# First-pass maxima and early projections of two sixteen-head attention stages placed in the mixture stage ahead

## The chip, the core and the metric

The kernel runs on one core of a Trainium2 chip. The metric is the device time of one execution in microseconds (us), the median of several. TensorE is PE in the profile (PEld its weight loads), VectorE is DVE, ScalarE ACT, GpSimd POOL, SyncE SP; SP issues nearly all DMAs.

## The reference

Twelve residual stages work on one activation x of 2048 tokens by 128 channels, in four layers: half a feed-forward, an attention, half a feed-forward. Each stage normalises x first.

```python
x = x + 0.5 * ffn(layernorm(x)); x = x + attn(layernorm(x)); x = x + 0.5 * ffn(layernorm(x))
```

Layer 0 (ffn0, attn0): capacity routing over 8 experts, causal attention with 8 heads of 16. Layer 1 (ffn1, attn1): every token goes through a shared and eight gated experts, `silu(x @ wg) * (x @ wu) @ wd`, weighted by a top-2 softmax; full attention with 16 heads of 8. Layer 2 (ffn2, attn2): x is quantised in blocks of 32 to a 6-bit float grid and multiplied by a quantised weight; full attention with 16 heads of 8 and rotary angles. Layer 3 (ffn3, attn3): ternary weights; causal attention with 16 heads of 64. The sixteen-head stages of this change are attn1 and attn2:

```python
attn = softmax(einsum('bqhd,bkhd->bhqk', q, k) * dh**-0.5); out = einsum('bhqk,bkhd->bqhd', attn, v) @ Wo
```

## The kernel before, in words

x lies in SBUF in four chunks of 512 tokens. Each stage is a Python generator `main` with a small `pre` that fetches weights. A tile scheduler orders the instructions of each engine by a simulated readiness and by the order in which they were traced; `tc.high_priority()` lifts instructions, `in_order` and `keep_in_program_order` (in flash: `pe`) pin them behind others. Each engine then runs its list strictly in order.

Overlap of stages is written by hand in `Stage`. `io.upcoming()` prepares the next stage (its pool in SBUF, its weights, its generator), `io.mark(c)` says that chunk c of x is final, and `io.lead(us)` takes us off what the next stage still owes (`due`); when nothing is owed, the next stage does one step, until it yields True ("led"). Pools grow from the left end of SBUF for even stages and from the right for odd ones.

The mixture `ffn1` goes over 4 chunks x 9 experts. For each expert `up` makes two double-bank products in PSUM, `pg` and `pu` (12 matmuls of 512 columns in all, with a high and low split), ACT makes the Silu (L715), DVE multiplies (L717); `down` of the expert before makes 16 matmuls (L725) and DVE adds them with the gate to x (L735). At expert 4 the `front` of the next chunk is made. `io.lead(4.3)` stands once in each expert of chunks 2 and 3. `pg`, `pu` and the first-pass scores `s1` of flash share one PSUM tag of two double banks (`banks`).

The attention of `packed` treats 4 heads as a group: 4 groups x 4 query chunks are 16 iterations of `flash`. Stream A (L1049 on) makes the first-pass scores of an iteration: for 4 row blocks and 4 key chunks two pairs each, 32 pairs of matmuls of 32 rows by 512 (L1069), each pair followed by a maximum over 512 keys (L1087, one DVE reduction for two heads). `put_max` then turns the maxima into two more rows of the query. Stream B makes the second-pass scores (L1190), exponentials (L1199) and the product with the values (L1136). B starts an iteration when A has finished it, so the first iteration's 32 reductions stand ahead of every exponential.

Before flash, `packed` makes for chunks 0 to 2, one chunk after another as x becomes final: `front` (normalise, transpose, split), `queries_or_keys(1, c)` (keys; the queries of chunk 0 too), each a step of a lead. In attn1 these steps fall into the mixture ahead (ffn1). In attn2 the stage ahead is `ffn2`, whose last chunk makes eight leads (`io.here()`), so they fall beside its last quantisation. Once the stage itself runs, `kms` and `qts` are allocated in the pool `att`, filled by POOL, and filled by DMA with the stacked high and low parts (`stack_k`, `stack_q`, L1379), and at the first maxima `hook` makes the last chunk's keys (L1330, L1331).

`ffn2` runs per chunk: layer norm on ACT, `quantised` (L776 to L793, mostly DVE), transpose, product, addition into x (L834). Its chunks 0 to 2 are led by ffn1.

Of the kernel before, what the change touches and what calls it, by code (L numbers as in the profile page):

```python
# [64 lines left out]
def tile_macaron(ctx: ExitStack, tc: tile.TileContext, a: dict, out: bass.AP, stages=STAGES):  # L65
# [598 lines left out]
    def ffn1(io, k, w, early):  # L664
# [35 lines left out]
        with tc.tile_pool(name="f1", bufs=1) as pool, tc.tile_pool(name="f1w", bufs=1) as pool_w:  # L700
# [42 lines left out]
            for c in range(NC):  # L743
                xT, gate = cur
                for n, e in enumerate(order):
                    h = up(e, xT)
                    if n + 2 < len(order):
                        expert(order[n + 2])
                    if last is not None:
                        down(*last)  # L750
                    last = c, e, h, gate
                    if n == 4 and c + 1 < NC:
                        cur = front(c + 1, pool)
                    if n == 0 and c:
                        io.mark(c - 1)
                    if c > 1:
                        io.lead(4.3)
                if c == 0:
                    io.upcoming()
# [3 lines left out]
    def quantised(src, pool, tag, bufs=1):  # L763
# [5 lines left out]
        def new(name, m=n):  # L769
            return pool.tile([P, m], F32, name=name, tag=tag + name, bufs=bufs)  # L770
# [25 lines left out]
    def pre_ffn2(k, pool):  # L796
        if k == 0:
            w = fetch(pool, "l2w", 0, C)
            wqT.append(const.tile([P, P], F32, name="wqT"))
            q = quantised(w, pool, "w")  # L800
# [6 lines left out]
    def ffn2(io, k, w, early):  # L807
        bufs = 2 if k == 0 else 1
        half_bias = early.tile([P, C], F32, name="half_bias")
        nc.vector.tensor_scalar_mul(half_bias, row("bias2"), 0.5)  # L810
        for c in range(NC):
# [7 lines left out]
            q = quantised(xn.rearrange("p i c -> p (i c)"), early, "x", bufs)  # L819
# [5 lines left out]
            qT = early.tile([P, CH], F32, name="qT", tag="qT", bufs=bufs)  # L825
# [9 lines left out]
            io.mark(c)  # L835
            if c < NC - 1:
                yield 1.0
                stats_of[c] = statistics_of(xs[c])

# [130 lines left out]
    def flash(io, pool, early, its, nh, causal, scale, s1, s2, pv_mm, put_max, begin, finish, poll=None,  # L970
              on_exp=None, split_at=1, fill=None, leads=None, hook=None, flush=True, order=None):
# [30 lines left out]
        if halved:  # L1002

            halves = {}
            for name in ("ident", "maskq", "maskk"):
                raw = pool.tile([P, 2, P], F32, name="halfraw", tag="halfraw", bufs=2)
# [5 lines left out]
                halves[name] = pool.tile([P, 2, P], BF16, name="half" + name)  # L1012
# [11 lines left out]
        if tiled and causal:  # L1024
            junk = pool.tile([P, CH], F32, name="junk")
            strip = pool.tile([P, CH], F32, name="strip")
# [22 lines left out]
        def stream_a():  # L1049
            for n, (g, qc) in enumerate(its):  # L1050
                begin(n)
                nk = chunks(qc)
                npair = (nk + 1) // 2
                mp = pool.tile([P, TC, nh, NC], F32, name="mp", tag="mp", bufs=3)
                for pi in range(npair):
                    for r in range(TC):
                        before = hook(n, pi, r) if hook is not None else None
                        if pi == r == 0 and before is None:
                            before = last_top.get(n - 1)
                        for kc in range(2 * pi, min(2 * pi + 2, nk)):  # L1060
                            for j0 in range(0, nh, 2):
# [14 lines left out]
                                with tc.high_priority():  # L1076
# [17 lines left out]
                mx = pool.tile([P, TC, nh], F32, name="mx", tag="mxa", bufs=3)  # L1094
# [140 lines left out]

        while alive[0] and pos[0] < end[0]:
            step_a()
# [58 lines left out]
    def packed(io, early, hd, causal, scale, project, w, wv, wo, bias=None):  # L1296
# [45 lines left out]

        for c in range(1 if causal else NC - 1):
# [8 lines left out]
            if causal:  # L1352
                values(c)
        yield True

        with tc.tile_pool(name="att", bufs=1) as pool, tc.tile_pool(name="far", bufs=1) as far:
            tops = []
# [3 lines left out]
            vts = []  # L1361
# [3 lines left out]
            os = [  # L1365
                (far if causal else early).tile([P, TC, C], F32, name=f"o{c}", tag=f"o{c}")
                for c in range(NC)
            ]

            n_km, n_qt = 2 * NC, 5 if causal else 3  # L1370
            kms = [pool.tile([P, nq, CH], F32R, name=f"km{i}") for i in range(n_km)]
            qts = [pool.tile([P, nq, CH], F32R, name=f"qt{i}") for i in range(n_qt)]
            km, qt, q2, vt = {}, {}, {}, {}
            turn, held_by = [0], []

            def rows_of(dst, srcs, o):

                for t, s in enumerate(srcs):
                    nc.sync.dma_start(  # L1379
                        out=dst.rearrange("(d t) n -> d t n", t=4)[:, t].bitcast(F32),  # L1380
                        in_=s[o : o + per * hd, :].bitcast(F32),
                    )

            def stack_k(g, c):
                t = kms[(g * NC + c) % n_km if not causal else g * NC + c]
                h, l = parts[c][1]
                for i in range(nq):
                    rows_of(t[:, i, :], (h, l, h), (g * nq + i) * per * hd)
                km[g, c] = t

            def stack_q(g, c):
                h, l = parts[c][0]
                t = qts[turn[0] % n_qt]
                turn[0] += 1
                held_by.append((g, c))
                assert turn[0] <= n_qt or held_by[-1 - n_qt] in q2
                for i in range(nq):
                    rows_of(t[:, i, :], (h, h, l), (g * nq + i) * per * hd)
                qt[g, c] = t

            def stack_v(g, c):
                vt[g] = vts[g % 2]
                nc.vector.tensor_copy(
                    slots(vt[g])[:, c * TC : (c + 1) * TC, :, :hd],
                    vall[c][:, :, g * 4 * hd : (g + 1) * 4 * hd].rearrange(
                        "p i (j d) -> p i j d", j=4
                    ),
                )

            if causal:  # L1410
                its = [(g, c) for c in range(NC) for g in range(n_groups)]
            else:
                its = [(g, c) for g in range(n_groups) for c in range(NC)]
            size = [((4 * c + 2.5) if causal else 4 * NC) * CH * 4 for _, c in its]
            leads = even(size) if causal else None
            keyed = [0]

            def steps_of(i):

                if not x_parts[i]:  # L1420
                    xn = layer_norm(i, False)
                    yield
                    front(i, xn)
                    yield
                    queries_or_keys(1, i)
                    if causal:
                        queries_or_keys(0, i)
                        yield
                        values(i)
                        yield  # L1430
                for g in range(2 if causal else 1):
                    stack_k(g, i)
                    if causal:
                        stack_v(g, i)
                        queue(its.index((g, i)))
                        yield

            def onward(c):

                if keyed[0] > c:  # L1440
                    return False
                if not making:
                    making.append(steps_of(keyed[0]))
                if next(making[0], True):
                    making.pop()
                    keyed[0] += 1
                return True

            making = []

            def ensure(c):
                while onward(c):
                    pass

            def queue(n):

                if n < len(its) and its[n] not in qt:
                    c = its[n][1]
                    if not parts[c][0]:
                        queries_or_keys(0, c)  # L1460
# [833 lines left out]
```

## Time and profile before

| | us |
|---|---|
| median of 3 runs | 3757.37 |
| lowest and highest | 3753.88, 3758.66 |
| profiled execution | 3769.46 |
| its span, first to last instruction | 3767.7 |
| first mixture, first to last Silu start | 638.5 to 810.9 |
| first exponentials of attn1 | 881.8 |
| second mixture, first to last Silu start | 1524.0 to 1696.6 |
| first exponentials of attn2 | 1788.4 |

Over the whole span PE is busy 91%, DVE 76%, ACT 54%, POOL 22%. In an answer by order of time a line gives the start, the length, the engine, the line of the program, the operation, what is written from what with its shape, and how many equal instructions were merged; in brackets stands how long the engine was idle before, and who released it. A busy PE is not PE at its peak. "PEclk" is the granted share of TensorE's full clock.

### The profile page before, as it was taken

What the parts mean: (1) busy time and instruction counts of PE and PEld (TensorE: products, weight loads), DVE (VectorE), ACT (ScalarE), POOL (GpSimd) and SP (SyncE); (2) the same over time, 40 slices, a digit from 0 to 9 for tenths busy, and PEclk for the clock granted to TensorE, in tenths of its full rate; (3) what the DMA queues carried; (4) which work ended last, traced back from release to release, by engine and by line L of the source; (5) the groups of instructions that cost most, each with busy time, mean ns of one, the idle gap of its engine ahead of it and who ended that gap; (6) DMA issues with size and microseconds to landing.
All of it is one profiled execution on the core that took longest, in us unless ns stands there. A gap on an engine that the chain in (4) does not pass through costs nothing. (4 is left out here: it accounts for less than half of the span.)

```text
span 3767.7 us, 64628 instructions
## 1 busy us (share of the span) xinstructions
PE 3420.8 (91%) x25325; PEld 1846.5 (49%) x25325; DVE 2870.9 (76%) x4793; ACT 2036.2 (54%) x3838; POOL 828.8 (22%) x830
## 2 busy tenths in 40 slices
PE   7679987978999999996999999888999999999989
PEld 5543356863333333783333333366444444444458
DVE  6488555768999998668899999654777877788862
ACT  3246732325888888421788888732333444444442
POOL 1511124110000000112000000142555445533341
PEclk9779988987999999996999999998899999999999
DMA  3311023000000000102000000012443232221010
GB/s 104 83 49 29 9 81 95 4 26 5 12 12 14 8 3 1 35 1 70 10 14 6 16 5 4 15 46 75 140 147 112 97 106 97 89 63 52 24 34 12
DMA packets 124689, 170.18 MB, mean 45 GB/s; under 512 B 25120, under 2 KB 52514, under 8 KB 124384
## 3 DMA queue, kind: packets, MB, share of 16 engines
q1 hardware_dynamic: 121824, 160.80, 13.7%
q0 software_dynamic: 2560, 5.25, 0.9%
q8 instruction: 199, 3.26, 0.3%
q14 instruction: 106, 0.87, 0.1%
HBM read 101.25 MB, written 45.87 MB: 39 GB/s over the span
## 5 line engine op out<-in xcount | busy, mean ns | idle before, releaser
L1087 DVE TENSOR_REDUCE mp<-s 128x2 f32<-128x1024 f32 (+3 forms) x1440 | 1625.7, 1181 | 88.5 <-PE s L1069 68.1
L1199 ACT ACTIVATE pt<-s 128x512 f32<-128x512 f32 (+1 forms) x2368 | 1220.7, 601 | 216.4 <-PE s L1190 141.8
L1190 PE MATMUL s<-q,km 32*128 32x512 f32 (+2 forms) x2368 | 733.6, 491 | 28.6 <-ACT pt L1199 18.7
L1136 PE MATMUL pv<-pt,v 128*32 128x256 f32 (+1 forms) x8568 | 730.9, 413 | 22.9 <-ACT ov L1577 11.2
L1069 PE MATMUL s<-km,qt 32*128 32x512 f32 (+3 forms) x2368 | 620.0, 507 | 61.1 <-DVE mp L1087 37.1
L1190 PEld LDWEIGHTS s<-q,km 32*128 32x128 f32 (+1 forms) x2368 | 324.1, 184 | 531.6 <-issue 341.3
L1179 ACT ACTIVATE pt<-s 128x512 f32<-128x512 f32 (+3 forms) x640 | 306.2, 530 | 355.7 <-PE s L1171 212.8
L143 POOL TENSOR_TENSOR rs<-rs,minus_half 128x4 f32<-128x4 f32 x56 | 57.5, 1026 | 1543.7 <-DVE rs L142 1542.7
L1993 DVE TENSOR_TENSOR sum<-sum,pt 128x512 f32<-128x512 f32 (+3 forms) x328 | 259.4, 805 | 89.9 <-ACT pt L1179 88.3
L1136 PEld LDWEIGHTS pv<-pt,v 128*32 128x32 f32 x8568 | 169.1, 108 | 316.4 <-issue 146.3
L1171 PE MATMUL s<-q,k 64*128 64x512 f32 (+3 forms) x1920 | 300.0, 403 | 14.7 <-ACT pt L1179 10.4
L1136 PE MATMUL pv<-pt,latv 128*64 128x512 f32 (+3 forms) x1280 | 310.4, 564 | 1.3 <-ACT pt L1179 1.3
L1993 POOL TENSOR_TENSOR sum<-sum,pt 128x512 f32<-128x512 f32 (+1 forms) x200 | 265.6, 1328 | 181.5 <-ACT pt L1179 177.0
L1069 PEld LDWEIGHTS s<-km,qt 32*128 32x128 f32 (+1 forms) x2368 | 236.4, 191 | 124.1 <-DVE mp L1087 82.3
L1171 PEld LDWEIGHTS s<-q,k 64*128 64x128 f32 x1920 | 161.8, 188 | 224.8 <-issue 137.3
L715 ACT ACTIVATE sg<-pg 128x1024 f32<-128x1024 f32 x72 | 73.9, 1027 | 174.4 <-PE pg L229 158.8
L1069 PE MATMUL s<-k,q 64*128 64x512 f32 (+3 forms) x640 | 133.7, 433 | 19.0 <-DVE mp L1087 18.6
L1791 DVE TENSOR_TENSOR rot<-rot,tab 128x512 f32<-128x512 f32 x128 | 87.7, 685 | 74.2 <-PE rot L229 38.4
L725 PEld LDWEIGHTS pd<-l1d,h 128*128 128x128 f32 x1152 | 139.3, 192 | 5.6
L725 PE MATMUL pd<-l1d,h 128*128 128x128 f32 x1152 | 140.1, 275 | 0.0
L717 DVE TENSOR_TENSOR h<-pu,sg 128x1024 f32<-128x1024 f32 x72 | 87.9, 1220 | 60.6 <-PE pu L229 55.7
L1171 PE MATMUL s<-q,two 64*128 64x512 f32 (+3 forms) x640 | 128.0, 368 | 0.0
(575 smaller groups left out, 4696.7 us busy)
## 6 DMA issues: line engine op xcount, KB each, us to landing
tab<-in_l3rope SPq DMA_DIRECT2D x66, 256.0 KB
q<-q SPq DMA_DIRECT2D x32, 512.0 KB
k<-k SPq DMA_DIRECT2D x32, 512.0 KB
l0e<-in_l0e SPq DMA_DIRECT2D x32, 256.0 KB
q<-h SPq DMA_DIRECT2D x32, 256.0 KB
q<-rot SPq DMA_DIRECT2D x32, 256.0 KB
k<-h SPq DMA_DIRECT2D x32, 256.0 KB
k<-rot SPq DMA_DIRECT2D x32, 256.0 KB
```

Of the source, the lines that this page charges most:

```text
L715: nc.scalar.activation(sg, pg, AF.Silu)
L717: nc.vector.tensor_tensor(h.rearrange("p m n -> p (m n)"), pu, sg, ALU.mult)
L725: nc.tensor.matmul(pd[:, i, :], h[:, m, i * P : (i + 1) * P], wd[:, m, :], start=m == 0, stop=m == 1,)
L1069: pe(nc.tensor.matmul(ps[:, o : o + w], lhsT, rhs[:, :w], start=True, stop=not masked))
L1087: ins = nc.vector.tensor_reduce(mp[:, r, j0 : j0 + 2, kc], both[:, :, :w], AX.X, ALU.max,)
L1136: i = pe(nc.tensor.matmul(pv[out_rows, lo:hi], lhsT, pts[j][:, lo:hi], start=kt == 0, stop=kt == nt - 1 and hi == CH))
L1171: pe(nc.tensor.matmul(outs[j][:, c0:], lhsT, rhs[:, c0:], start=i == 0, stop=i == len(terms[0]) - 1 and not diag,))
L1179: ex = nc.scalar.activation(pts[j][:, c0:], outs[j][:, c0:], AF.Exp, scale=scale)
L1190: pe(nc.tensor.matmul(ps[:, c0:], lhsT, rhs[:, c0:], start=i == 0, stop=i == len(terms) - 1 and (tiled or not diag),))
L1199: ex = nc.scalar.activation(pt[:, c0:], ps[:, c0:], AF.Exp, scale=scale)
L1791: nc.vector.tensor_tensor(t.bitcast(F32), ps, halves["tabs"][i], ALU.mult)
L1993: eng.tensor_tensor(t[:, c0:], other[:, c0:], pts[j][:, c0:], ALU.add)
```

## The change

1. `ffn1` leads twice in each expert of chunks 1, 2 and 3, with 3.2 each, instead of once with 4.3 in chunks 2 and 3.
2. `lead` serves the next two stages instead of one, and preparing the first ffn2 prepares attn2 too. So ffn1 leads ffn2 and, as ffn2's chunks are marked, attn2.
3. `flash` is a generator and takes `ahead`: that many steps of stream A are made, each followed by a yield, before the rest. For attn1 and attn2 it is 24 of the first iteration's 32: one step is one pair of matmuls with its reduction. The first iteration goes key chunk by key chunk instead of by pairs of key chunks; its pairs made ahead have no high priority.
4. In `packed`, after chunk c's keys the lead stacks them (and chunk 0's queries) by DMA, owes 3.0, and then makes 8 pairs, owing 1.0 for each; chunk 1's queries are made early too. Three of the key tiles and one query tile are allocated in the stage's early pool for it.
5. attn2 takes the left end of memory (as ffn2 does), the two ffn2 stages share one pool, and `quantised` has single buffers, with the transposed result in the place of `big`. attn2's weights are fetched in two parts.
6. With flash a generator, key and query tiles are allocated and filled alternately, in attn0 too; ffn2 marks a chunk behind its statistics instead of ahead.

Most other lines of the diff move functions of `packed` out of the `with`, unchanged. Its core:

```diff
@@ ffn1
-                    if c > 1:
-                        io.lead(4.3)
+                    if c:
+                        io.lead(3.2)
...
+                    if c:
+                        io.lead(3.2)
@@ ffn2
-            qT = early.tile([P, CH], F32, name="qT", tag="qT", bufs=bufs)
+            qT = early.tile([P, CH], F32, name="qT", tag="xbig", bufs=1)
@@ flash, stream_a
-                npair = (nk + 1) // 2
-                mp = pool.tile([P, TC, nh, NC], F32, name="mp", tag="mp", bufs=3)
-                for pi in range(npair):
-                    for r in range(TC):
-                        before = hook(n, pi, r) if hook is not None else None
+                if n == 0 and ahead:
+                    mp = early.tile([P, TC, nh, NC], F32, name="mp0")
+                    turns = [(r, [kc]) for kc in range(nk) for r in range(TC)]
+                else:
+                    mp = pool().tile([P, TC, nh, NC], F32, name="mp", tag="mp", bufs=3)
+                    turns = [
+                        (r, range(k0, min(k0 + 2, nk))) for k0 in range(0, nk, 2) for r in range(TC)
+                    ]
...
-                                with tc.high_priority():
+                                with tc.high_priority() if not leading[0] else nullcontext():
@@ flash
+        leading = [True]
+        for _ in range(ahead):
+            step_a()
+            yield
+        leading[0] = False
@@ packed
+        def hook(n, kc, r):
...
+            if n == 0 and kc == NC - 1:
+                if r == 0:
+                    with tc.high_priority():
+                        ensure(NC - 1)
+                if r == 1:
+                    queue(1)
+                    values(0)
+                    stack_v(0, 0)
...
+        flow = flash(..., ahead=0 if causal else 2 * TC * (NC - 1))
+        if not causal:
+            new_k(early)
+            new_q(early)
         for c in range(1 if causal else NC - 1):
...
+            stack_k(0, c)
+            keyed[0] = c + 1
+            if c == 0:
+                stack_q(*its[0])
+            if c + 2 < NC:
+                new_k(early)
+            yield 3.0
+            for _ in range(2 * TC):
+                next(flow)
+                yield 1.0
+            if c == 1:
+                queries_or_keys(0, c)
+                yield 1.5
         yield True
@@ Stage
-            if self.n + 1 < len(line):
-                s = line[self.n + 1]
+            for s in line[self.n + 1 : self.n + 3]:
                 s.due -= passed
                 if s.steps is not None and not s.led and s.due <= 0.0:
                     s.step()
+    between = [n for n in range(1, len(stages)) if stages[n - 1] == ("ffn2", 0)]
+    def side_of(n):
+        return sides[n % 2 if n not in between else (n - 1) % 2]
```

## The prediction

> **What bounds the kernel now.** I read three views in this order: busy time by stretch around the two stages with sixteen heads, the order of time at the start of the first of them, and the order of time at one place where its matmuls already stand among full-size ones. The stretches first (length, then busy us and instruction count of PE, weight loads, DVE, ACT, POOL, then granted clock, DMA share, GB/s):
>
> ```profile
> core 0: us, PE busy (x) PEld busy (x) DVE busy (x) ACT busy (x) POOL busy (x), PEclk, DMA share, GB/s
> 722.00:815.80 93.80, 93.04 (x583) 82.40 (x581) 60.23 (x158) 28.56 (x33) 6.94 (x6) 1.00 0.02 5
> 815.80:837.00 21.20, 5.58 (x22) 4.36 (x22) 10.00 (x22) 5.75 (x12) 7.49 (x13) 0.66 0.19 49
> 837.00:882.00 45.00, 30.53 (x84) 11.21 (x80) 42.79 (x41) 2.11 (x3) 0.00 (x0) 0.50 0.08 21
> ...
> 1580.00:1701.50 121.50, 120.10 (x766) 106.78 (x765) 87.77 (x250) 36.25 (x43) 12.53 (x11) 1.00 0.00 1
> 1701.50:1741.00 39.50, 21.44 (x63) 14.05 (x61) 27.90 (x68) 11.90 (x24) 17.01 (x23) 0.61 0.35 105
> 1741.00:1788.00 47.00, 31.11 (x94) 12.70 (x94) 45.38 (x47) 3.30 (x5) 2.56 (x2) 0.57 0.17 52
> 2400.00:2450.00 50.00, 39.92 (x236) 17.12 (x228) 27.33 (x97) 35.66 (x72) 14.76 (x13) 0.86 0.09 27
> 2500.00:2550.00 50.00, 44.37 (x201) 34.60 (x200) 26.21 (x59) 17.35 (x25) 17.56 (x21) 0.97 0.10 32
> ```
>
> Rows 1 and 4 are the two mixtures: PE is full, DVE has 28% to 36% free. Rows 2, 3 and 5, 6 are what follows each: a chain with every engine mostly idle (21 and 40 us), then a stretch in which DVE alone is full (45 and 47 us) and ACT does nothing. That stretch is the first iteration's maxima:
>
> ```profile
> 836.57 0.80 PE L1069 MATMUL s<-km,qt 32*128 32x512 f32 x4 [6.54 <-issue]
> 837.40 36.29 DVE L1087 TENSOR_REDUCE mp<-s 128x2 f32<-128x1024 f32 x32 [5.97 <-PE s L1069]
> ```
>
> 32 reductions in 36.29 us, 1.13 us each; exponentials can only begin behind them: the first score matmul of the second pass starts at 880.5. In the second stage with sixteen heads it starts at 1787.1.
>
> **What leaves the path, attn1.** The mixture's last addition ends at 817.4. The last chunk's chain (statistics, normalisation, transposes, keys) ends with kL at 830.3 and stays. Its three key DMAs issue at 0.6 us apiece, so keys land near 834; today the maxima start at 836.6, behind query DMAs that stand late in SP's queue and that the change issues during the mixture. Then 8 reductions instead of 32: 8 x 1.13 = 9.1, to about 843. From the maxima's end to the first second-pass matmul takes 880.5 - 873.7 = 6.8 us, so about 850 instead of 880.5: **31 us** gained (27 if the maxima start no sooner, 33 if the POOL memsets, 11 of 512 columns today and 7 in the new place, also free the normalisation, which took 4.83 us there against 1.1 elsewhere).
>
> **What leaves the path, attn2.** Here the last chunk's quantisation stands among the attention's early projections of chunks 0 to 2 (ffn2's own chunks 0 to 2 are in the mixture already: the quantisation's POOL subtraction is there three times). From its first reduction to its addition into x it takes 1709.4 to 1732.2, 22.8 us; in the next ffn2 an undisturbed chunk takes 2408.9 to 2419.6, 10.7 us. With the projections gone 12 us come back. From that addition to the key's high half is 11 us (1732.2 to 1743.3), kL and DMAs some 4 more, then 9.1 of maxima and 6.8: 1720 + 11 + 4 + 9 + 7 = 1751 against 1787: 36 us; some of the last chunk's query work remains beside it, so I take **35** (31 to 37).
>
> **What enters the mixtures.** Per mixture 24 pairs of first-pass matmuls and 24 reductions. What a pair costs PE among full-size matmuls, the trace shows once at full clock:
>
> ```profile
> 1742.16 0.39 PE L228 MATMUL rot<-xL,w1H 128*128 128x512 f32 x1
> 1742.38 0.40 PE L229 MATMUL rot<-xH,w1L 128*128 128x512 f32 x1
> 1742.71 0.50 PE L1069 MATMUL s<-km,qt 32*128 32x512 f32 x2
> 1743.14 0.94 PE L1338 MATMUL bank<-l2a,vall 128*128 128x128 f32 x6
> ```
>
> Full-size matmuls follow each other every 0.23 us, so without the pair the next would have started at 1742.61; it starts at 1743.14: 0.53 us for a pair whose two matmuls run side by side in 0.23. The Trainium skill's "TensorEngine Tiling (Array Packing)", Key Properties, says what the rest is: going between the 32-row and the full arrangement of the array drains it first. That speaks against this change: the pairs are laid singly between full-size matmuls, so each pays it twice. By the stream alone 48 pairs cost 11 us, by the row 25.
>
> Above that, pairs share PSUM's two double banks with the mixture's gate and up products (one tag, two buffers). With two pairs in an expert of 4.52 us (the spacing of undisturbed Silu activations), the up product of the next expert gets its bank only when the second reduction is done. By hand, from the end of an up product: h to 1.5, first reduction to 2.7, the four gated additions (4 x 0.28) to 3.85, second reduction to 5.03, up product until 6.5: 2.0 us more per expert, 1.0 per pair. If the second reduction goes ahead of the additions it is only the drains. Bounds per pair 0.23 and 1.4 (a whole reduction and the drains); I take **0.65**, near the 0.53 row, because PE is what the mixture runs on and the additions can give way: 24 x 0.65 = 15.6 us per mixture.
>
> DVE has room for it: the first mixture gets 24 x 1.16 = 28 us from chunk 1 on. The second gets 28 and the early projections' 3 x 1.8 + 5 x 2.07 = 16 (normalisation 1.1 and xL 0.69; two products with the tables and a low half, 0.69 each): 88 + 44 = 132 us in some 146. That is 90%, close enough that I add **3 us** of collisions (0 to 10). PE there also gets 3 transposes at 0.66 and 5 projections of 6 matmuls at 0.23: **8.9 us**; in the first mixture only one query projection is new (3 x 0.23 = **0.7**).
>
> The leads' other instructions: each moved chunk brings three key DMAs (chunk 0 three query DMAs too, in attn2 also rope tables) on SP, 0.6 us of issue each. Behind them on SP stand only each other and the next chunk's: the nine experts' weights are all fetched in chunk 0, DMA share in rows 1 and 4 is 0.02 and 0.00. Cost 0; had the weights stood behind a DMA that waits for kL, it would be several us per expert. The pairs are pinned on PE behind what was traced before them, so a late key DMA would hold a pair, but mixture matmuls may pass. ACT gets two evictions of 0.6 per projection at 30% load: 0.
>
> **The small edits.** attn2 in the left end of memory, both ffn2 in one pool, single quantisation buffers: chunks of a mixture are 41 us apart and a quantisation takes 11, so a single buffer is long free. The ternary weights' load waits for attn2's end today (2439.2; its consumer waits 1.6 us): from -3 to +3, taken as 0. In the causal attention memsets of keys and queries alternate: 11.7 us of POOL in all as before, +-2, taken as 0.
>
> A second rule speaks against it. The skill's "TensorE: Matmul & The Clock Gate", A second HAM failure mode, tells of a kernel that cycles through PSUM banks, where short waits of PE let the clock fall again and again. Here rows 7 and 8 are nearest: PE at 89% busy has clock 0.97, at 80% 0.86. With 5.8 us per expert PE stays above 90%, so by the row the clock costs under 3%, a microsecond or so; by the rule at half clock the 24 affected experts' 4.52 us would double, some 100 us. I go by the row.
>
> **Sum.** attn1: 31 - 15.6 - 0.7 = 14.7. attn2: 35 - 15.6 - 8.9 - 3 = 7.5. Together **22 us**. The profiled execution took 3769.46 us (span 3767.7 and 1.8 around it), 12 us over the median of 3757.37; the sum would bring it to 3747. Nothing in the steps scales with that 0.3%, so I take 22 from the median: **3735**.
>
> **Rivals.** (1) *The bank decides, and it is slower.* Every pair costs a whole reduction and both drains, 1.13 + 0.3 = 1.43: 48 x 1.43 = 69, with 12.6 of the rest 81 against 66: 15 slower, 3772. For it: one tag with two buffers, and the hand count of 1.0 per pair. Against: a reduction needs PE to wait only if DVE is behind, and DVE has a quarter free. It turns at (66 - 12.6) / 48 = 1.11 us per pair. (2) *Drains are hidden* behind waits that are there anyway: 0.23 per pair, 66 - 11 - 9.6 = 45, 3712. For it: in the flash stages pairs and value matmuls alternate at 98% DVE. Against: the row above. (3) *The pairs come late*: without high priority they slide to the mixture's end, so that half of the 66 us remains on the path while the projections' PE time is still paid: about 0, 3757. For it: the front of the next chunk falls into the same experts. Against: three free experts of 4.5 us stand behind the last chunk's pairs in the first mixture.
>
> **Chances.** The forecast (3728 to 3745 for pairs at 0.5 to 0.85) 0.50; rival 2 0.13; rival 3 0.15; rival 1 0.22. About 0.2% (7.5 us) is what a measurement here can tell from no change. Faster 0.64, same 0.15, slower 0.21. The range, 3714 to 3770, takes in nearly all of rivals 1 and 2.
>
> **What would show it.** Right: 24 of the first 32 reductions under each mixture; between the last gated addition and the first second-pass matmul some 32 us instead of 63 in attn1 and 50 instead of 85 in attn2; mixtures longer by about 16 and 28 us, with Silu spacings near 5.8 where pairs stand. Wrong: spacings of 7 and more with PE waiting on the reduction (rival 1), a clock below 0.9 in the mixtures, or reductions bunched behind the mixture's end (rival 3).

## The result and the profile after

The changed kernel takes **3807.19 us** (median of 4, 3802.52 to 3810.55) against 3758.01 for the kernel before beside it: ratio 1.0131, 95% interval 1.0114 to 1.0149. It is 49 us slower, where 22 us faster was predicted. The profiled execution took 3802.52 us, span 3800.7.

First the busy time by stretch, columns as in the table of the prediction; the kernel before, its two mixtures:

```profile
638.50:811.90 173.40, 170.09 (x1049) 149.09 (x1048) 125.42 (x380) 55.51 (x61) 22.27 (x20) 1.00 0.04 11
1524.00:1697.60 173.60, 170.43 (x1063) 149.94 (x1062) 126.28 (x354) 54.38 (x66) 26.51 (x23) 1.00 0.07 20
```

And the changed kernel: each mixture, then the chain behind it, then the maxima that are left, up to the first exponential.

```profile
623.90:832.00 208.10, 191.53 (x1100) 157.27 (x1100) 153.96 (x405) 55.62 (x62) 24.13 (x24) 0.97 0.05 13
832.00:852.00 20.00, 9.00 (x53) 7.35 (x51) 9.77 (x26) 5.17 (x11) 5.60 (x9) 0.79 0.15 36
852.00:869.20 17.20, 11.12 (x32) 4.35 (x32) 15.41 (x16) 1.86 (x2) 0.00 (x0) 0.50 0.11 27
1510.90:1762.90 252.00, 213.63 (x1159) 174.03 (x1157) 175.92 (x429) 61.10 (x77) 39.04 (x38) 0.92 0.11 33
1762.90:1799.50 36.60, 12.98 (x62) 9.72 (x60) 17.22 (x50) 7.56 (x17) 9.12 (x12) 0.63 0.17 45
1799.50:1816.70 17.20, 11.12 (x32) 4.35 (x32) 15.41 (x16) 1.84 (x2) 0.00 (x0) 0.50 0.01 4
```

The tails did what was said. From the mixture's last Silu to the first exponential it is 37.2 us instead of 69.9, and 53.8 instead of 90.8. In the order of time on DVE the maxima of attn1 are eight:

```profile
852.01 9.14 DVE L1096 TENSOR_REDUCE mp<-s 128x2 f32<-128x1024 f32 x8 [3.32 <-PE s L1078]
```

The mixtures are what went wrong: 208.1 us instead of 173.4, and 252.0 instead of 173.6. In the second PE stands idle for 38 of its 252 us; neither it nor DVE (176) is full.

The time by stage, from the start of a stage's first Silu or exponential to the end of its last, from two pairs of profiles. The second pair (e17_before_third and e18_after_again, one run each, 3767.48 and 3827.42) was taken on one chip:

| us | before | after | before | after |
|---|---|---|---|---|
| start to first exponential | 220.4 | 210.8 | 221.5 | 221.9 |
| attn0's exponentials | 245.3 | 245.4 | 246.4 | 245.8 |
| to the first mixture | 172.8 | 167.7 | 172.2 | 172.8 |
| first mixture | 173.5 | 208.1 | 173.4 | 205.9 |
| to attn1's exponentials | 69.8 | 37.3 | 69.9 | 37.2 |
| attn1's exponentials | 638.8 | 638.2 | 637.4 | 637.4 |
| second mixture | 173.6 | 252.0 | 173.8 | 252.8 |
| to attn2's exponentials | 90.8 | 53.8 | 90.5 | 53.8 |
| attn2's exponentials | 647.6 | 649.0 | 652.3 | 654.4 |
| to attn3's exponentials | 212.9 | 217.2 | 212.9 | 218.9 |
| attn3's exponentials | 969.7 | 968.0 | 963.0 | 972.1 |

The mixtures add 111 to 113 us, the tails give 69.5, and 4 to 6 are lost ahead of attn3. That is 48 in each pair, near the 49 of the medians. As whole spans the first pair shows only 33, because its two kernels start differently, which goes with the chip (see the end), and the second shows 60, 9 of them in attn3's exponentials, which differ as much between profiles of one kernel.

Where the time goes inside the second mixture is read on PE in order of time, between a Silu at 1574.86 and the next at 1610.76:

```profile
1579.28 0.40 PE L229 MATMUL pu<-xTH,wgu3L 128*128 128x512 f32 x1
1583.93 1.15 PE L180 MATMUL turn<-cst,xn 128*128 128x128 f32 x4 [4.26 <-DVE xn L166]
1584.88 3.37 PE L725 MATMUL pd<-l1d,h 128*128 128x128 f32 x16
1588.00 0.47 PE L227 MATMUL rot<-xH,w2H 128*128 128x512 f32 x1
...
1591.40 0.39 PE L229 MATMUL rot<-xH,w1L 128*128 128x512 f32 x1
1591.63 1.95 PE L725 MATMUL pd<-l1d,h 128*128 128x128 f32 x16
1595.90 0.66 PE L180 MATMUL turn<-cst,xn 128*128 128x128 f32 x4 [2.33 <-DVE rot L1729]
...
1599.74 0.47 PE L180 MATMUL turn<-cst,xn 128*128 128x128 f32 x1 [2.43 <-DVE xn L166]
1601.12 1.88 PE L678 MATMUL bank<-l1d,x2T 128*128 128x8 f32 x8 [0.90 <-DVE x2T L674]
1602.85 3.76 PE L725 MATMUL pd<-l1d,h 128*128 128x128 f32 x16
1606.54 0.79 PE L1078 MATMUL s<-km,qt 32*128 32x512 f32 x2
1607.26 0.80 PE L227 MATMUL pg<-xTH,wgu4H 128*128 128x512 f32 x1
```

For 28 us no gate or up product runs. PE walks down a chain with a wait at each link (10.6 us in all): attention's transposes, its two projections (12 matmuls), the transposes and logits of the next chunk's front, then the pair, and directly behind the pair the gate product of expert 4. Between the waits it is slow: 16 down products take 1.95 us at full clock, but 3.37 and 3.76 here, where the mean granted clock is 0.82 (1571 to 1610). Such a stretch stands once in each of the three chunks (35.9, 30.7 and 23.3 us from Silu to Silu).

### The profile page after: what moved, and what is told of

The parts are those of the page before. It is cut to its first block, busy times and chain, and to the rows that moved or that the text cites. A ratio compares the mean times of both kernels' runs of the same rounds, so it can differ in the third digit from the quotient of the medians.

```text
span 3800.7 us, 64638 instructions
## 1 busy us (share of the span) xinstructions
PE 3428.8 (90%) x25325; PEld 1849.6 (49%) x25325; DVE 2877.9 (76%) x4793; ACT 2035.8 (54%) x3838; POOL 828.1 (22%) x830
## 5 line engine op out<-in xcount | busy, mean ns | idle before, releaser
L1208 ACT ACTIVATE pt<-s 128x512 f32<-128x512 f32 (+1 forms) x2368 | 1220.5, 601 | 219.6 <-PE s L1199 162.9
L1078 PE MATMUL s<-km,qt 32*128 32x512 f32 (+3 forms) x2368 | 605.9, 497 | 57.5 <-DVE mp L1096 18.7
L1188 ACT ACTIVATE pt<-s 128x512 f32<-128x512 f32 (+3 forms) x640 | 306.2, 530 | 354.2 <-PE s L1180 210.8
L143 POOL TENSOR_TENSOR rs<-rs,minus_half 128x4 f32<-128x4 f32 x56 | 57.4, 1026 | 1510.8 <-DVE rs L142 1510.5
L1180 PE MATMUL s<-q,k 64*128 64x512 f32 (+3 forms) x1920 | 298.1, 402 | 16.0 <-ACT pt L1188 11.2
L2035 POOL TENSOR_TENSOR sum<-sum,pt 128x512 f32<-128x512 f32 (+1 forms) x200 | 265.0, 1325 | 180.0 <-ACT pt L1188 172.2
L725 PE MATMUL pd<-l1d,h 128*128 128x128 f32 x1152 | 154.4, 287 | 0.0
L725 PEld LDWEIGHTS pd<-l1d,h 128*128 128x128 f32 x1152 | 148.3, 201 | 11.9 <-issue 6.4
```

Source lines behind the costliest of these rows:

```text
L725: nc.tensor.matmul(pd[:, i, :], h[:, m, i * P : (i + 1) * P], wd[:, m, :], start=m == 0, stop=m == 1,)
L1078: pe(nc.tensor.matmul(ps[:, o : o + w], lhsT, rhs[:, :w], start=True, stop=not masked))
L1180: pe(nc.tensor.matmul(outs[j][:, c0:], lhsT, rhs[:, c0:], start=i == 0, stop=i == len(terms[0]) - 1 and not diag,))
L1188: ex = nc.scalar.activation(pts[j][:, c0:], outs[j][:, c0:], AF.Exp, scale=scale)
L1208: ex = nc.scalar.activation(pt[:, c0:], ps[:, c0:], AF.Exp, scale=scale)
L2035: eng.tensor_tensor(t[:, c0:], other[:, c0:], pts[j][:, c0:], ALU.add)
```

## The experiments

All stage times below are measured as in the table; "mixtures" are the two mixtures, "tails" the stretches behind them. The runs were made on several chips, so their times are compared by the ratio, which is to the kernel before on the same chip.

| run | mixtures | tails | time | ratio to before (95%) |
|---|---|---|---|---|
| before | 173.5, 173.6 | 69.8, 90.8 | | |
| changed | 208.1, 252.0 | 37.3, 53.8 | 3807.19 | 1.0131 (1.0114 to 1.0149) |
| e1_no_pairs | 177.4, 201.2 | 63.9, 78.4 | 3774.97 | 1.0056 (1.0039 to 1.0073) |
| e3_own_bank | 207.8, 234.2 | 37.2, 59.3 | 3795.77 | 1.0123 (1.0090 to 1.0157) |
| e4_later | 205.0, 222.8 | 38.0, 57.4 | 3776.53 | 1.0060 (1.0040 to 1.0080) |
| e5_unpinned | 205.3, 253.3 | 37.2, 53.9 | 3803.22 | one run |
| e7_ready_pairs | 204.4, 244.7 | 63.7, 79.2 | 3845.02 | 1.0239 (1.0222 to 1.0256) |
| e8_lane | 209.0, 251.0 | 37.2, 53.9 | 3805.41 | 1.0140 (1.0122 to 1.0159) |
| e9_lane_later | 196.8, 219.5 | 37.0, 57.1 | 3765.74 | 1.0023 (1.0009 to 1.0037) |
| e10_lane_no_pairs | 176.0, 195.8 | 62.6, 78.9 | 3766.82 | 1.0028 (1.0018 to 1.0038) |
| e11_ready_unpinned | 198.5, 229.0 | 63.9, 79.2 | 3821.05 | 1.0174 (1.0150 to 1.0197) |
| e12_attn1_only | 196.2, 175.4 | 37.3, 96.3 | 3756.72 | 1.0006 (0.9995 to 1.0017) |
| e13_graft | 196.0, 173.9 | 37.3, 90.8 | 3762.76 | 0.9983 (0.9975 to 0.9991) |
| e15_graft_both | 196.0, 173.4 | 37.3, 88.8 | 3749.18 | 0.9979 (0.9965 to 0.9992) |
| e16_price | 196.8, 218.5 | 63.3, 80.3 | 3808.69 | 1.0146 (1.0120 to 1.0173) |

The theory at first: a led step is traced before its operands are ready, PSUM banks are handed out in the order of tracing, and so the mixture's own products wait for a bank behind it. The rival: the pairs' drains and reductions crowd PE and DVE.

**Without the pairs**, e1_no_pairs (early projections and stacked keys stay):

```diff
+        early_pairs = False
...
-            ahead=0 if causal else 2 * TC * (NC - 1),
+            ahead=2 * TC * (NC - 1) if early_pairs else 0,
...
-            for _ in range(2 * TC):
+            for _ in range(2 * TC if early_pairs else 0):
                 next(flow)
                 yield 1.0
```

> The changed kernel, without the 24 pairs made ahead in both stages; the early projections, the stacks of keys and the two leads per expert stay. The changed kernel's mixtures take 208 and 252 us from first to last Silu, the kernel's before 173 and 174; the stretches from a mixture's last Silu to the first exponential take 37 and 54, before 70 and 91. Head of line (a step of a lead that is traced before its operands are ready holds a PSUM bank, and the mixture's own products queue for it): the first mixture returns to 174 to 183; the second keeps part of its excess, since the projections of attn2 still follow the quantisation's chain in the banks that the down products use: 185 to 215. The tails grow to about 66 and 72. In all 3750 to 3785. Crowding (the pairs' own PE and DVE time is the cost): both mixtures at 174 and 183 or so, 3735 to 3755.

The pairs are 30.7 us of the first mixture's excess and 50.8 of the second's. But the second keeps 27.6 us with no pair in it: the early projections, put at 11.9, cost more than twice that. The tails shortened by 5.9 and 12.4; the 12 that the prediction gave to the undisturbed quantisation are there.

**Another bank, later, not pinned.** Three edits of the changed kernel, each alone:

```diff
@@ e3_own_bank: two single products instead of a pair
...
+                                        ps = held("s1")
+                                        lhsT, rhs = s1(n, j0 + j, r, kc)
+                                        pe(nc.tensor.matmul(ps, lhsT, rhs, start=True, stop=True))
@@ e4_later
-            yield 3.0
+            yield 16.0
             for _ in range(2 * TC):
@@ e5_unpinned: of the pairs made ahead
-                                    pe(nc.tensor.matmul(
+                                    mm = nc.tensor.matmul(
...
+                                    if not leading[0]:
+                                        pe(mm)
```

> The changed kernel, with the pairs made ahead replaced by single products of 512 columns, each in a PSUM bank that the mixture does not use (the value product's), each with its own reduction; everything else as changed. Head of line: gate and up products no longer wait for a pair's bank, so the first mixture falls from 208 to about 190; in the second only the part of the stalls that the pairs make goes, since down products still share three banks with transposes, projections and ffn2's product: about 252 to 210-225. In all 3750 to 3785. Crowding (drains and reductions are the cost; single products drain as often or oftener): the mixtures stay at 208 and 252 or grow, 3800 to 3830.

> The changed kernel, with 16.0 us owed behind the stacking of a chunk's keys instead of 3.0, so that the pairs are traced later, when their keys have landed. Head of line: the gap at the first pair of each chunk closes in both mixtures; the first falls from 208 to about 192, the second from 252 to 215-230; some pairs of the third chunk are traced at or behind the end of the mixture and make its tail a few us longer; in all 3755 to 3790. Crowding: the same number of pairs costs the same wherever they stand, 208 and 252 stay, 3800 to 3815.

> The changed kernel, with the first-pass matmuls that are made ahead no longer pinned on PE behind what was traced before them. Pinning as the cause (the pin keeps a pair ahead of mixture products that are ready): the gaps of 23 to 36 us in the second mixture go, which falls from 252 to below 215, and the first from 208 to about 185. Head of line by the banks: the hand-out of banks stays as it was traced, so 208 and 252 stay within 5 us, and the time within 10 us of the changed kernel's 3807.

Neither theory came through whole. Own banks took 18 us from the second mixture and nothing from the first. But that is the sum of two things, for 24 pairs had become 48 single products. The two mixtures of that run:

```profile
625.80:833.60 207.80, 202.48 (x1100) 156.67 (x1100) 156.14 (x429) 55.58 (x62) 24.09 (x24) 1.00 0.05 13
1514.80:1749.00 234.20, 211.46 (x1140) 165.14 (x1139) 171.89 (x444) 60.93 (x76) 39.33 (x38) 0.98 0.12 35
```

PE stands idle for 5.3 and 22.7 us, in the changed kernel for 16.6 and 38.4, without pairs for 5.4 and 15.5. So most of the wait went with the shared bank, although the singles stand just as late and as pinned as the pairs did: it is the double bank handed to the pair first that puts the gate product behind it. The 24 more products took this back in the first mixture, at (207.8 - 177.4) / 48 = 0.63 us each. PE in order of time there:

```profile
798.83 0.40 PE L227 MATMUL pg<-xTH,wgu2H 128*128 128x512 f32 x1
799.15 0.49 PE L1075 MATMUL s<-km,qt 32*128 32x512 f32 x1
799.57 0.50 PE L228 MATMUL pg<-xTL,wgu2H 128*128 128x512 f32 x1
799.91 0.40 PE L229 MATMUL pg<-xTH,wgu2L 128*128 128x512 f32 x1
```

The starts follow each other at 0.32, 0.42 and 0.34 us, where without the single two steps of 0.23 would stand: a single costs 0.62, about what a pair costs in an undisturbed expert (0.60, below), and far more than the 0.23 in which 512 columns stream. The second tile of a pair is nearly free. That fits what the Trainium skill's "TensorEngine Tiling (Array Packing)", Key Properties, says of the drain; no run here varies the columns. Later tracing took 29 us from the second mixture and 3 from the first. In the first, pairs were now traced just behind the next chunk's front. PE in order of time in that kernel (its lines as in the changed one):

```profile
695.25 1.04 PE L180 MATMUL turn<-cst,xn 128*128 128x128 f32 x8
697.97 1.06 PE L678 MATMUL bank<-l1d,x2T 128*128 128x8 f32 x8 [1.68 <-DVE x2T L674]
698.96 0.50 PE L1078 MATMUL s<-km,qt 32*128 32x512 f32 x2
699.39 0.65 PE L227 MATMUL pg<-xTH,wgu4H 128*128 128x512 f32 x1
```

The pair stands behind the front's logits, which wait for DVE, and the gate product behind the pair; Silu to Silu takes 11.2 us there against 5.4 without pairs. The pin alone was worth 3 us and nothing.

**Ready operands**, e7_ready_pairs. To the kernel without pairs, 24 pairs per mixture were added on a constant and an expert's weights:

```diff
...
+                        ps = banks("s1")
...
+                            tc.keep_in_program_order(nc.tensor.matmul(
+                                ps[:, j * CH : (j + 1) * CH], masks_b["ident_r"][rows_j, :],
+                                long_ready[0][rows_j, :], start=True, stop=True,
+                            ))
+                        nc.vector.tensor_reduce(spare[...], ..., AX.X, ALU.max)
```

> The kernel without pairs made ahead, to which 24 pairs per mixture are added, at the places, in the banks and with the reductions of the changed kernel's pairs, but on operands that are ready long before (a constant and an expert's weights); their maxima are not used, so all 32 real ones stay behind the mixture. It prices a pair that never waits for its operands. Without pairs the mixtures took 177 and 201 us, with the changed kernel's pairs 208 and 252. If the price is drains and streaming, 0.65 us a pair: 193 and 217. If crowding makes the whole excess (1.28 and 2.1 us a pair): 208 and about 250. If a ready pair costs nothing beside the stream, 0.23: 183 and 207. Total: 3775 plus what the mixtures gain over 177 and 201, so 3807, 3855 or 3787.

Late keys are not the cause alone: pairs that wait for nothing cost nearly the same, 27.0 and 43.5 us. Here the pin still holds them behind the chain. Cutting it as well, e11_ready_unpinned:

> As the run with 24 added pairs per mixture on ready operands (mixtures of 204.5 and 244.7 us, 3845), but these matmuls are not pinned on PE behind what was traced before them: now neither a key nor the pin holds a pair. (Unpinning alone changed nothing, and ready operands alone changed little.) Order: a pair has to stand behind the led chain on PE, by its keys or by the pin, and the gate and up products behind the pair, which is handed a bank first; with both ties cut the pairs stand ahead of the chain, the gaps of 33, 31 and 18 us in the second mixture go, and it takes 212 to 225; the first, whose pairs at ready operands stood closer, 195 to 203; total 3805 to 3825. Crowding, or the drains, as the price: 204 and 245 stay, 3840 to 3850.

21.1 and 27.8 us remain of 30.7 and 50.8. Keys alone cut 3.7 and 7.3, the pin alone 2.8 and -1.3, both 9.6 and 23.0: either tie is enough to put a pair behind the led chain in PE's fixed order. The 21.1 us in the first mixture, 0.88 a pair, are a first price of a pair alone: this run and the one without pairs differ in nothing else. In the second mixture gaps of 22, 20 and 14 us stayed, so the order behind these pairs is not all.

**The banks of the down products.** Transposes, projections and ffn2's product of the led steps in the idle bank, with pairs (e8_lane) and without (e10_lane_no_pairs):

```diff
     def bank(name="bank"):
+        if aside[0]:
+            return held(name)
...
+            aside[0] = not causal and not io.here()
             front(c)
+            aside[0] = False
```

> The changed kernel, with the led steps' transposes, projections and the quantised product in the value product's PSUM bank, which a mixture leaves idle, instead of the three banks that the down products use; pairs and leads as changed. Head of line by the three banks (down products queue behind led steps whose operands are late, and the up products run out of h buffers): the gaps of 23 to 36 us in the second mixture go, and it falls from 252 to 210 to 225; the first, whose loss is at the pairs' bank, stays at 200 to 208; total 3765 to 3785. Crowding: 208 and 252 stay, 3807.

> The kernel without pairs made ahead, with the led steps in the value product's bank. Head of line by the three banks: of the 24 us by which the second mixture is longer than the first (201 against 177) what is left is PE's own time for projections and transposes, 8.9, and some collisions: 184 to 192, total 3757 to 3766. If the projections' own work makes the 24: 201 stays, 3775. First mixture 177 in both.

This part of the first theory fell: with pairs 209.0 and 251.0, unchanged. Without pairs it gave 1.4 and 5.4. The three banks do not hold the mixture; what stands behind the pair's own bank in PE's order does.

**All three edits for the waits** (the third is the idle bank above), with the real pairs (e9_lane_later), and then with ready, unpinned ones (e16_price):

```diff
-            yield 3.0
+            yield 16.0
...
-                    if c:
+                    if c and n != 4:
                         io.lead(3.2)
```

> The changed kernel with three edits for the waits: led steps in the value product's bank, 16.0 owed behind the stacking instead of 3.0, and no lead directly behind the next chunk's front, where pairs were traced behind its gate product. Head of line: what stays is a pair's drains and stream (24 x 0.65) and the projections, so mixtures of 193 to 198 and 203 to 212, tails of 38 to 45 and 54 to 60, total 3735 to 3760, even with or faster than the kernel before. Crowding: mixtures of 205 and 223 or more as with the later pairs alone, 3776.

> As the run with added pairs on ready operands, not pinned, and with the three edits for the waits (led steps in the idle bank, 16.0 owed ahead of the pairs, no lead behind the front): the nearest to a pair's own price. Without pairs, with the idle bank, the mixtures took 176 and 196 us. At the 0.65 us a pair that the prediction took: 192 and 212, total 3767 + 32 = 3799. If a pair's own price is the whole excess of the changed kernel over the kernel without pairs (1.28 and 2.1 us): 207 and 246. If it is a whole reduction and two drains, 1.43: 210 and 230.

The real pairs with all three edits still lose 0.2%, a little more than expected, but both runs give the same mixtures within 1 us, 196.8 and 219.5 against 196.8 and 218.5, so with these edits the real pairs no longer wait for anything that ready ones don't. What is left over 176.0 and 195.8 is taken as the price of a pair: 20.8 / 24 = 0.87 and 22.7 / 24 = 0.95 us, above the 0.65 taken, far below 1.28 and 2.1. The place, 11.3 and 33.5 us, was the rest. Two of the three edits are not in the run without pairs, so this price holds what they do without pairs too; in the first mixture the 0.88 from above agrees. In the second one expert of e16_price still takes 20.2 us, without pairs 12.9 at most, so its 0.95 holds some waiting.

**A version that gains.** Pairs only in attn1, with the three edits; then only that on top of the kernel before; then attn0 in its changed form too:

```diff
@@ e12_attn1_only, ffn1
-                    if c:
+                    if c > 1 and k:
+                        io.lead(4.3)
+                    if c and not k and n != 4:
                         io.lead(3.2)
@@ e13_graft, on the kernel before
 def attn1
-        yield from packed(io, early, 8, False, ...)
+        yield from packed_ahead(io, early, 8, False, ...)
@@ e15_graft_both
 def attn0
-        yield from packed(io, early, 16, True, ...)
+        yield from packed_ahead(io, early, 16, True, ...)
```

> Pairs ahead only in the first stage with sixteen heads, with the three edits for the waits (led steps in the idle bank, 16.0 owed behind the stacking, no lead behind the front); the second stage is led as before the change (one lead of 4.3 in each expert of chunks 2 and 3, for the next stage alone, no pairs), with all its memory as in the changed kernel. By the stage sums of the run with the same edits in both stages, the first mixture with its tail takes 234 instead of 243 us, a gain of 9.5; the second with its tail is as before, 264; some 4 us are lost between the second stage's end and the last stage's exponentials, as in all runs of the changed kind. Sum: 3744 to 3753, faster than both kernels if the 4 us are not larger. If the gain of the first stage came from the second stage's changes or the pair's price is larger alone: 3755 to 3765.

> The kernel before, with nothing but the first sixteen-head stage taken from the run with pairs in that stage alone (24 pairs ahead, led steps in the idle bank, 16.0 owed, no lead behind the front); the second stage, both quantised stages, memory and all order there are the kernel's before. That run gained 9.8 us in the first mixture with its tail, and by its stages lost 7.3, 5.3 and 4.4 us in the second tail, the second stage's exponentials and the stretch behind them. If those losses belong to the other edits of the change: 3742 to 3750, faster than both kernels. If the 9.8 us in one profile are the kernel before's own slow start and spread: 3753 to 3760.

> The graft (the kernel before with the first sixteen-head stage taken over, 0.9983 of the time before), with the causal attention of layer 0 also in the changed form (key and query tiles filled alternately, the flash function a generator). In the kernel before, its second profile and the graft the first exponential comes at 218 to 222 us and the first mixture 171 to 173 behind that attention's end; in the changed kernels at 209 to 213 and 165 to 168. If these 15 us come with the causal attention's new form: 210 and 166, and 0.993 to 0.995 of the time before. If they come with where the whole program lies and not with that stage: 218 to 222 and 172 stay, 0.997 to 0.999.

attn1 by itself gains: mixture and tail take 233.3 to 233.5 instead of 243.3. With the change's other edits (e12_attn1_only) that is spent again (5.5 in the second tail, 4.4 ahead of attn3), and the expected gain did not come; grafted on the kernel before, it makes the kernel **faster than both**, 0.9983 and 0.9979, 5 to 7 us. The second ratio is no better than the first although its profile begins the first mixture 16 us earlier (623.9 and 640.2).

**The start.** The kernel before and the changed one once more:

> The kernel before once more, for a second profile: the first one was 12 us over its median, and its first exponential came at 220.4 where every later kernel has 209 to 213. If those 12 us were lost ahead of the first mixture, it now begins near 626 instead of 638.5, and mixtures, tails and exponentials measure as in the first profile within 2 us: 173, 70, 639, 174, 91, 648, 213.

> The kernel before a third time, beside the changed kernel on the same chip. If the late start belongs to the chip, first exponential and the stretch behind the first attention agree between the two kernels within 2 us (either 218 to 222 and 171 to 173 in both, or 209 to 213 and 165 to 168 in both). If it belongs to the change, the kernel before keeps 218 to 222 and 171 to 173 and the changed one 209 to 213 and 165 to 168.

> The changed kernel again, beside the kernel before on the same chip; see the run beside it. Mixtures, tails and exponentials as in its first profile: 208, 37, 638, 252, 54, 649.

The last two answer it: on one chip both kernels start late (221.5 and 221.9, then 172.2 and 172.8). The 15 us do not belong to the change. The expectation for the second profile of the kernel before (one run, 3761.0) was wrong: it started late again (218.0, then 170.6).

## Why the prediction was wrong

**What leaves the path: right.** Between the last gated addition and the first second-pass matmul it is 30.5 us (837.5 to 868.0) where 32 was said, and 47.6 (1767.9 to 1815.5) where 50 was said. The tails gave 32.5 and 37.0 for 31 and 35; eight reductions took 9.14 for 9.1.

**What enters the mixtures: wrong, three times.** In steps from the kernel before to the one without pairs (e10_lane_no_pairs), from there to the one with ready pairs (e16_price), and on to the changed one, the excess is:

| us | predicted | first mixture | second mixture |
|---|---|---|---|
| early projections and leads | 0.7, 11.9 | 2.5 | 22.2 |
| a pair's own price, x24 | 15.6 each | 20.8 | 22.7 |
| place in PE's order | 0 | 11.3 | 33.5 |
| sum | 16.3, 27.5 | 34.6 | 78.4 |

That is 69 us more than said, 45 of it by the place, 12 by the price and 12 by the projections. With 3.5 more gained in the tails and some 5 lost ahead of attn3 it turns 22 faster into 49 slower.

The step that failed is the sentence "a late key DMA would hold a pair, but mixture matmuls may pass". They could not: PE runs one list in order, and behind the pair stand the gate products, whose double banks are handed out behind the pair's; with products in another bank most of the wait was gone. The step was costed by its instructions (PE 0.23, DVE 1.13), not by the latency of the chain that it ends. The chain takes from the transposes at 1583.9 to the pair at 1606.5, five experts of 4.52 us, while the owed 1.5, 1.5 and 3.0 are paid within one or two experts, which credit 6.4 each. With 16.0 owed instead of 3.0, 3.1 and 29.2 us of it went; with the idle bank and no lead behind the front as well, all that ready pairs do not pay.

**The pair's price** was the right mechanism and a third too small. Where two pairs stand in an undisturbed expert the spacing is the 5.8 that was said. ACT in order of time, changed kernel:

```profile
804.68 1.03 ACT L715 ACTIVATE sg<-pg 128x1024 f32<-128x1024 f32 x1 [7.87 <-PE pg L229]
810.41 1.03 ACT L715 ACTIVATE sg<-pg 128x1024 f32<-128x1024 f32 x1 [4.71 <-PE pg L229]
816.14 1.03 ACT L715 ACTIVATE sg<-pg 128x1024 f32<-128x1024 f32 x1 [4.70 <-PE pg L229]
```

5.73 against 4.52 is 0.60 a pair. The mean of 0.87 to 0.95 is higher because of other experts: in the first mixture two pairs make the one that holds the next chunk's front 8.5 us instead of 6.8, and the one behind it, which catches up, 5.8 instead of 3.2. **The early projections** were counted in matmuls, 8.9 us. Of their 22 PE is busy 12.0 us longer and idle 10.2 us longer (182.4 of 195.8 us without pairs in the idle bank, 170.4 of 173.6 before); the idle part, waits of PE for the led chain's other engines, had no term. The "3 us of collisions on DVE" can't be told apart: DVE is busy 76% with ready pairs (165.6 of 218.5), where 90% was feared.

**The rules.** The cost around a change of arrangement was real, as the single products show. The clock cost more than the microsecond that was taken. It was 0.97 and 0.92 over the mixtures, 0.82 and 0.76 over the two longest gaps, and behind one the next matmuls start every 0.4 to 0.6 us instead of 0.23 (1607.26 to 1608.54). From the changed kernel to the one with all three edits, the same pairs at clocks of 1.00 and 0.98, PE's idle time falls by 6.5 and 17.0 us (16.6 to 10.1, 38.4 to 21.4) and its busy time by 4.8 and 15.4 (191.5 to 186.7, 213.6 to 198.2). So nearly half of the place is PE working more slowly. An estimate from the granted clock gives as much: 0.08 of 252 us is 20, 0.02 of 219.6 is 4. In kind the rule set aside was right, in size a fifth of the 100 us. Here the low clock goes with the gaps and goes when they go.

**The rivals.** Rival 1 had the sign but not the cause: a ready pair costs 0.87 to 0.95 us on the mean, below the 1.11 at which it turns, and the place makes the rest. Rivals 2 and 3 are out; all 24 maxima stood under each mixture. The values of rivals 1 and 2, 3772 and 3712, lie just outside the range that was to take in nearly all of them. The sign named for a wrong prediction, spacings of 7 and more and a clock below 0.9, is what came, the clock in gaps and not in every expert.

**Open.** Why in the second mixture ready, unpinned pairs still had gaps of 14 to 22 us, and one of 20 when traced later, and which of the other edits costs the 4 to 6 us ahead of attn3 (small differences all along that stretch).

## What to carry to other kernels

A step that is slipped into another stage costs what it holds up on each in-order engine, not only its own instructions: ask what stands directly behind it in that engine's list and how long its operands take to come, and let it owe that latency. Here the same pairs cost 1.70 us apiece traced at once (81.5 us for 48 over the run without pairs), 1.03 (49.2 for 48) traced 16 owed us later, and 0.93 (44.5 for 48, over the run without pairs in the same bank) with all three edits. Price the place first. Then see what is left: a pair takes 1.13 us of reduction off the path and gives back four fifths of it in the stage that it fills, which leaves a few us per stage (10 in attn1, with what the lead brings besides), and nothing where other waits come with it.

## What was not expected of the hardware

A stage that no edit touches differed by 15 us between chips. In layer 0's routed experts PE stands without anything that the profile shows; the kernel before, PE in order of time, and the first graft at the same place:

```profile
113.20 0.31 PE L229 MATMUL bank<-xdH,ew1sL 128*128 128x320 f32 x1
120.64 0.63 PE L227 MATMUL bank<-xdH,ew1sH 128*128 128x320 f32 x1 [7.13 <-issue]
```

```profile
117.58 0.64 PE L231 MATMUL bank<-xdH,ew1sH 128*128 128x320 f32 x1 [4.96 <-issue]
```

In the first profile of the changed kernel the matmuls run on without a gap there; on the chip of its second one the stretch is as late as in the kernel before. For the changed kernel the chip decides it. The kernel before has no profile with an early start, but its times agree: medians of 3753 to 3756 us on two chips where all profiles start early, 3770 on one where they start late. What PE waits for is not shown. So a sum by stages from two profiles needs a common start. And the last stage's exponentials take 960 to 970 us in three profiles of one and the same kernel.
